# Layer 1's attention: first query inside the last expert step, activation tables asked for earlier, PSUM banks reordered and released singly

## The chip, the cores and the metric

The kernel runs on one core of a Trainium2 chip. The metric is the device time of one execution in microseconds; the time of a kernel is the median of several runs. A separate execution is recorded by the hardware profiler, and all profile lines come from that one. The core has five engines that work side by side, each in its own order: TensorE (PE, with its weight loads as PEld), VectorE (DVE), ScalarE (ACT), GpSimd (POOL) and SyncE (SP), which here only starts transfers. They wait for each other on semaphores.

## The reference

The input x has 8 batches of 512 tokens with 512 features, in fp32. Two layers follow, each an attention and a feed-forward block; after every block the sum of block and input is normalised over the features:

```python
x = _layernorm(x + L0_attn(x))   # causal softmax attention, 16 heads of 32, biases
x = _layernorm(x + L0_ffn(x))    # 8 experts, top 2 of a softmax router, LoRA on all weights
x = _layernorm(x + L1_attn(x))   # no mask, 8 query heads of 64 in 2 groups of one key/value head; returns x + out @ Wo.T
x = _layernorm(x + L1_ffn(x))    # silu(x Wg) * (x Wu), then Wd; weights are integers (w - 128) * scale, 1408 hidden
```

In layer 1's attention the scores are `softmax(q k^T / sqrt(64))`. An expert computes `silu(gate) * up` on 256 hidden features and projects them down to 512.

## The kernel before, in words

**Layer 0's attention** (`attention0`) goes through the batches in turn, and in each through four groups of four heads. A group is three units of scores: the scores on TensorE, Exp on ScalarE (L1470), the causal mask as a select on GpSimd (L1480), the product with v on TensorE (`av`, L1497), and the running sum of p on VectorE (L1505). At a group's end TensorE sums over the keys (`rs`, L1512), ScalarE copies that to `r_inv` (L1074), VectorE takes the reciprocal (L1515) and multiplies (L1516), and GpSimd adds the inverses into a guard, `g_total` (L1077). Once a batch GpSimd also adds a bias row to x (L1589).

**The experts.** Tokens are gathered into tiles of 128 by expert. `Tiles.step` (L1012) is the pipeline: step i starts the gate and up matmuls of a later tile, transposes the hidden values of tile i (`turn_hidden`, L968: two transposes into `ps_hT`, a copy to `hT` on ScalarE), and multiplies them by the down weights (`down`, L978: four passes into `ps_y`, a copy to `y` on ScalarE or VectorE, and a DMA from SP to `results`). The loop in `usual_pass` calls `step` and then a piece of other work meant for that step (`beside`), among them the pieces of layer 1's attention for batch 0: its gathers, sums and norm, its key, its value and, as the last piece, its first query (`query`, L1717: eight passes into `ps_q`, a copy to `qT`, L1724). After the loop, `rare` (L1036) has each engine read a tile count, `t_n_free` (L1039), and branch (L1041): extra tiles are computed only in the unusual case, which doesn't occur in this run.

**Layer 1's attention** (`Attention1.run`, `batches`) starts behind that branch. SP loads the rows of batches 2 to 7 (`load_rows`, L1954, two DMAs of 512 KB a batch); GpSimd gathers the expert results of the next batch (`yr`, L722), and VectorE adds them to x with their weights (L729). The attention itself is a stream of units: scores (two heads at a time, in banks of the pool `p_sc`), Exp to `p` on ScalarE (L1818), sums over the key tiles on VectorE (`total`, L1826), the product with v (`av`, L1837), and at a group's end `rs` (L1845, in a bank of the pool `p_mm`), the copy `r_inv` (L1074), reciprocal (L1848) and `aoT` (L1855). The projection with Wo (`ps_o`) is followed by the residual on VectorE (L1790), the statistics (L1798, L1799), `rstd` on GpSimd (L1802, L1803) and the norm (L1809).

For the last batch there is no next one beside which the projection could stand. Its four token tiles get four banks; each is first projected over three of the four groups, then over the last group, with residuals and then statistics behind (L1919 to L1934). The first two banks come from `p_mm`, the other two from `p_sc`.

**Layer 1's feed-forward** (`IntegerFfn.run`, L1191) opens its PSUM pools `d_gu` and `d_o` on the banks that the attention has given back, and computes for every chunk of 128 hidden features `ps_g` and `ps_u` (L1222), `sg` by Silu on ScalarE (L1225), `hT` on VectorE (L1227), its high and low halves (cast on ScalarE L1232, difference on VectorE L1233) and the down matmuls `ps_f` (L1238). The integer weights are converted on VectorE a slice at a time (L1137).

**What sets the order.** Inside `in_order(...)` blocks the named engines execute in the order in which the program issues their work: VectorE, ScalarE, GpSimd and SP in the loop over the expert steps, VectorE, ScalarE and GpSimd in layer 1's attention. Elsewhere a scheduler orders the instructions by their dependences. A tile pool with `reuse_waits="tile"` makes the first user of a place wait for the users of just that place; without it, for the last user of all the places that the pool takes over.

Of the kernel before, what the change touches and what calls it, by code (L numbers as in the profile page):

```python
# [9 lines left out]
F32 = mybir.dt.float32  # L10
# [3 lines left out]
AF = mybir.ActivationFunctionType  # L14
ALU = mybir.AluOpType
AX = mybir.AxisListType
PSUM = bass.MemoryType.PSUM

P = 128
NB = 8  # L20
S = 512
# [46 lines left out]
def in_order(tc, *engines):  # L68


    return tc.manual_schedule(engines={mybir.EngineType.PE, *engines})
# [43 lines left out]
class Env:  # L115
# [19 lines left out]
    def open_stream(self, ctx, batches, **kw):  # L135

        resident = ctx.enter_context(self.tc.tile_pool(name=f"resident{batches[0]}", bufs=1, **kw))
        for b in batches:
            self.xs[b] = resident.tile([P, NT, D], F32, tag=f"x{b}", name=f"x_{b}")
# [687 lines left out]
class Tiles:  # L827
# [181 lines left out]
        for i in range(2, 4):  # L1009
            self.turn_rows(i, self.nc.scalar.copy)  # L1010

    def step(self):  # L1012
        i = self.next
        self.next += 1
        if i == 0:
            self.down(i)
        if i + 2 < N_FIXED:
            self.half(i + 2)
        elif N_FIXED <= i + 1 < self.n:
            self.gate_up(i + 1, lambda: self.turn_hidden(i))  # L1020
        elif i + 1 == self.n:
            self.turn_hidden(i)
        if i + 8 < self.BY_BLOCKS:
            self.fetch(i + 8)
        if i + 10 >= self.BY_BLOCKS:
            self.fetch(i + 10)
        if i:
            self.down(i)
        for n in (4, 5) if i == 0 else (5,):
            if i + n < self.BY_BLOCKS:  # L1030
                self.turn_rows(i + n)
        if i + 6 >= self.BY_BLOCKS:
            self.pair_back(i + 6)
        if i + 7 >= self.BY_BLOCKS:
            self.blocks(i + 7)
# [109 lines left out]
class IntegerFfn:  # L1145
# [45 lines left out]
    def run(self, held_out, last_norm):  # L1191
        tc, nc, weights = self.env.tc, self.nc, self.weights
        with ExitStack() as phase:
            self.work = phase.enter_context(tc.tile_pool(name="d_work", bufs=1))
            self.p_gu = phase.enter_context(tc.tile_pool(name="d_gu", bufs=2, space=PSUM))
            self.p_o = phase.enter_context(tc.tile_pool(name="d_o", bufs=1, space=PSUM))
            weights.open(phase.enter_context(tc.tile_pool(name="d_weights", bufs=1)), 3 * NHID - weights.at)
            self.sd = self.work.tile([P, D], F32, name="sd")
            with tc.tile_pool(name="d_slots", bufs=1) as slots:
                while weights.at < 3 * NHID:  # L1200
                    weights.load(slots, 4, 3 * NHID)
                    weights.convert()
                nc.sync.dma_start(out=self.sd, in_=self.env.ins.s_down.partition_broadcast(P))
            with tc.tile_pool(name="d_raw", bufs=1) as self.raw:
                for b in range(NB - 1):
                    self.batch(b)
                    if b == 0:
                        last_norm()
                        ps = self.p_gu.tile([1, 1], F32, tag="g", name="ps_held")
                        nc.scalar.dma_start(out=held_out, in_=self.guard.partitions_held(self.env.const, ps))  # L1210
            self.late = phase.enter_context(tc.tile_pool(name="d_late", bufs=self.HELD))
            self.batch(NB - 1)
# [437 lines left out]
class Attention1:  # L1650
# [78 lines left out]
    def first_pieces(self):  # L1729

        do = self.first = self.prepare(0)

        def fetch(t):
            do["fetch"](t)
            self.scale(t)

        def blocks(tiles):
            for t in tiles:
                do["blocks"](t)

        return ([lambda t=t: fetch(t) for t in range(NT)] + [lambda t=t: do["add"](t) for t in range(NT)]
                + [do["deviations"], do["norm"], lambda: blocks((0, 1)), lambda: blocks((2, 3)), lambda: None, lambda: None]
                + [do["key"], do["value"], lambda: do["query"](0)])

    def scale(self, c):

# [12 lines left out]
    def batches(self, work, p_sc, p_av, weights, split):  # L1759
        env, nc, guard, state, HD = self.env, self.nc, self.guard, self.state, self.HD  # L1760
# [2 lines left out]

        state[0]["aoT"] = work.tile([P, ND, S], F32, tag="aoT", name="aoT1", bufs=2)
        weights.load(work, 2, weights.FIRST)

        w_out = work.tile([P, ND, 512], F32, name="attn1_out")
        for j in range(2):
# [6 lines left out]
        pieces = {0: self.first}  # L1775
# [7 lines left out]
        def project_groups(b, t, ps, groups):  # L1783
            for c in groups:
                self.multiply(1, ps, state[b]["aoT"][:, c, ts(t, P)], w_out[:, c, :], c)
# [136 lines left out]
        banks = [self.mm([P, D], "ps_o1")]  # L1922
        project_groups(b, 0, banks[0], range(ND - 1))
        sums[-1]()
        banks.append(self.mm([P, D], "ps_o1"))
        banks += [p_sc.tile([P, 2, S], F32, tag="sc", name="ps_o1")[:, 0, :] for _ in range(2)]
        for t in range(1, NT):
            project_groups(b, t, banks[t], range(ND - 1))
        norm(b - 1)
# [8 lines left out]
def usual_pass(tc, ins, held_out):  # L1938
    nc = tc.nc
    with ExitStack() as ctx:  # L1940
        env = Env(ctx, tc, ins)
        guard = Guard(env)
        keep = ctx.enter_context(tc.tile_pool(name="routed", bufs=1, side="right"))
        dram = ctx.enter_context(tc.tile_pool(name="routed_rows", bufs=1, space=bass.MemoryType.DRAM))
        with tc.tile_pool(name="a_mm", bufs=2, space=PSUM) as p_mm, ExitStack() as attn1_ctx:
            with tc.tile_pool(name="routes", bufs=1, side="right") as routes, \
                    tc.tile_pool(name="experts", bufs=1, side="right") as pool, ExitStack() as tiles_ctx:
                experts = Experts(env, pool, dram)
                router, tiles, tables = attention0(env, guard, keep, routes, experts, dram, p_mm, tiles_ctx)

                def load_rows(b):
                    for t in range(0, NT, GAP // P):
                        rows = router.rows[router.row_at(b, t) :][:GAP]
                        nc.sync.dma_start(out=env.xs[b][:, t : t + GAP // P, :], in_=rows.rearrange("(t p) d -> p t d", p=P))  # L1954

                env.open_stream(ctx, range(2))
                rows = ctx.enter_context(tc.tile_pool(name="c_rows", bufs=1))
                own = attn1_ctx.enter_context(tc.tile_pool(name="c_own", bufs=1))
                attention = Attention1(env, guard, router, rows, own, p_mm, dram)
                beside = {tiles.next + 6 * (b + 1): lambda b=b: load_rows(b) for b in range(2)}  # L1960

                for i, piece in enumerate(attention.first_pieces()):
                    beside[E * NT + 4 + 2 * i] = piece
                with in_order(tc, mybir.EngineType.DVE, mybir.EngineType.Activation, mybir.EngineType.Pool,
                              mybir.EngineType.SP):
                    while tiles.next < tiles.n:
                        tiles.step()
                        next(tables, None)
                        beside.pop(tiles.next, lambda: None)()
                assert not beside and next(tables, None) is None  # L1970
                tiles.rare()
            env.open_stream(ctx, range(2, NB), side="right")
            for b in range(2, NB):
                load_rows(b)
            weights = IntegerWeights(env, guard)
            pool = ctx.enter_context(tc.tile_pool(name="c_weights", bufs=1, side="right"))
            weights.open(pool, weights.FIRST)
            pool.tile([P, 56], F32, name="c_aligned")
            ffn = IntegerFfn(env, guard, weights, rows, dram)
            last_norm = attention.run(weights, ffn.split)  # L1980
        ffn.run(held_out, last_norm)
# [223 lines left out]
def post_ln_two_layers(tc, *aps):  # L2205

    nc = tc.nc  # L2210
    ins = Inputs(*aps)
    with tc.tile_pool(name="flag", bufs=1, space=bass.MemoryType.DRAM) as dram:
        held = dram.tile([1, 1], I32, name="held_out")
        usual_pass(tc, ins, held)
        count = nc.values_load(held[0:1, 0:1], min_val=0, max_val=P, skip_runtime_bounds_check_because="a count of partitions")
        with tc.If(count < P):
            general_pass(tc, ins)
# [70 lines left out]
```

## Time and profile before

| | us |
|---|---|
| median of 3 runs (2122.55 to 2125.76) | 2122.95 |
| the profiled execution | 2119.8 |
| its span, first to last instruction | 2118.1 |
| TensorE busy | 2080.9 |
| VectorE busy | 1269.7 |
| ScalarE busy | 606.6 |
| GpSimd busy | 498.2 |

The granted TensorE clock is 0.997 of full speed. Three places of the span matter for what follows: about 50 to 62 us (batch 0 of layer 0's attention), about 1071 to 1094 us (the last expert tile and the start of layer 1's attention), and about 1603 to 1630 us (the end of that attention and the start of the feed-forward block).

A line of a timeline has the start and the length in us, the engine, the source line and operation, what is written and read, and the number of instructions put together; in brackets stands how long the engine was idle before it and what it then waited for. A line of the waits has the engine and what waited, then what for, the us in total, the number of times and the longest. A line about DMA has the number of transfers, the size of each and the median time from issue to landing.

### The profile page before, as it was taken

What the parts mean: (1) busy time and instruction counts of PE and PEld (TensorE: products, weight loads), DVE (VectorE), ACT (ScalarE), POOL (GpSimd) and SP (SyncE); (2) the same over time, 40 slices, a digit from 0 to 9 for tenths busy, and PEclk for the clock granted to TensorE, in tenths of its full rate; (3) what the DMA queues carried; (4) which work ended last, traced back from release to release, by engine and by line L of the source; (5) the groups of instructions that cost most, each with busy time, mean ns of one, the idle gap of its engine ahead of it and who ended that gap; (6) DMA issues with size and microseconds to landing.
All of it is one profiled execution on the core that took longest, in us unless ns stands there. A gap on an engine that the chain in (4) does not pass through costs nothing. (4 is left out here: it accounts for less than half of the span.)

```text
span 2118.1 us, 35841 instructions
## 1 busy us (share of the span) xinstructions
PE 2080.9 (98%) x15114; PEld 1051.5 (50%) x15114; DVE 1269.7 (60%) x1963; ACT 606.6 (29%) x838; POOL 498.2 (24%) x489
## 2 busy tenths in 40 slices
PE   9999999999999999999999999999999999999997
PEld 2333333333334677774433333333334888888886
DVE  3667676776767633224247898887867644555443
ACT  2333323323323111111133333333332322222222
POOL 2343534434333211232042222223101000000000
PEclk9999999999999999999999999999999999999999
DMA  9020303414222447777561322132102311111000
GB/s 323 22 73 29 101 19 108 144 47 155 82 100 101 134 140 225 231 237 210 155 208 50 100 71 80 50 100 80 41 1 70 100 40 60 60 60 60 21 20 22
DMA packets 170588, 208.16 MB, mean 98 GB/s; under 512 B 61851, under 2 KB 115099, under 8 KB 167347
## 3 DMA queue, kind: packets, MB, share of 16 engines
q1 hardware_dynamic: 159136, 170.10, 25.6%
q0 software_dynamic: 10560, 34.61, 5.5%
q8 instruction: 122, 2.00, 0.4%
q10 hardware_dynamic: 722, 1.07, 0.1%
q14 instruction: 48, 0.39, 0.1%
HBM read 129.96 MB, written 75.78 MB: 97 GB/s over the span
## 5 line engine op out<-in xcount | busy, mean ns | idle before, releaser
L1077 POOL TENSOR_TENSOR g_total<-g_total,r_inv 128x512 f32<-128x512 f32 x64 | 90.1, 1408 | 487.3 <-DVE r_inv L1848 269.9
L1470 ACT ACTIVATE p<-sc 128x2048 f32<-128x2048 f32 (+1 forms) x96 | 153.0, 1593 | 178.9 <-PE sc L65 155.3
L1505 DVE TENSOR_TENSOR p<-p 128x1536 f32<-128x1536 f32 (+2 forms) x96 | 149.9, 1562 | 80.3 <-POOL p L1480 70.2
L1227 DVE SCALAR_TENSOR_TENSOR hT<-ps_u,vec,sg 128x512 f32<-128x512 f32 x88 | 65.6, 746 | 188.9 <-PE ps_u L1222 188.9
L1238 PE MATMUL ps_f<-ffn_w,h_half 128*128 128x512 f32 x672 | 169.8, 393 | 2.6 <-DVE h_half L1233 2.0
L957 PE MATMUL ps_gu<-xrT,experts 128*128 128x256 f32 x736 | 166.7, 380 | 0.0
L957 PEld LDWEIGHTS ps_gu<-xrT,experts 128*128 128x128 f32 x736 | 139.2, 191 | 31.9 <-issue 15.6
L1818 ACT ACTIVATE p<-sc 128x1024 f32<-128x1024 f32 x128 | 124.2, 1022 | 99.3 <-PE sc L65 99.3
L1848 DVE RECIPROCAL r_inv<-r_inv 128x512 f32<-128x512 f32 x32 | 107.1, 3346 | 67.6 <-ACT r_inv L1074 67.6
L1238 PEld LDWEIGHTS ps_f<-ffn_w,h_half 128*128 128x128 f32 x672 | 124.5, 188 | 34.6 <-DVE h_half L1233 7.6
L1222 PE MATMUL ps_g<-x_high,ffn_w 128*128 128x512 f32 x352 | 137.3, 390 | 0.8 <-DVE x L1790 0.8
L1222 PE MATMUL ps_g<-x_low,ffn_w 128*128 128x512 f32 x352 | 137.2, 390 | 0.0
L1222 PE MATMUL ps_u<-x_low,ffn_w 128*128 128x512 f32 x352 | 137.2, 390 | 0.0
L1222 PE MATMUL ps_u<-x_high,ffn_w 128*128 128x512 f32 x352 | 137.1, 389 | 0.0
L65 PE MATMUL sc<-qT,kT 64*64 64x512 f32 x1024 | 124.7, 602 | 1.1 <-ACT qT L1724 0.7
L65 PE MATMUL ps_q<-experts 128*32 128x512 f32 x1024 | 120.8, 601 | 4.8 <-DMA experts<-in_xT 4.4
L1480 POOL TENSOR_SCALAR_AFFINE_SELECT p<-p 128x512 f32<-128x512 f32 x128 | 82.7, 658 | 165.1 <-ACT p L1470 155.5
L65 PE MATMUL ps_v<-experts 128*32 128x512 f32 x1024 | 120.9, 595 | 0.0
L1837 PE MATMUL av<-p,v 128*64 128x512 f32 x512 | 120.9, 594 | 0.0
L65 PE MATMUL ps_o<-attn_out,aoT 128*64 128x512 f32 x512 | 116.4, 598 | 0.8 <-ACT r_inv L1074 0.8
L65 PE MATMUL ps_k<-experts 128*32 128x512 f32 x1024 | 116.3, 595 | 0.0
L65 PE MATMUL ps_q<-hT,attn_qkv 128*64 128x512 f32 (+1 forms) x504 | 116.2, 596 | 0.0
(277 smaller groups left out, 3198.0 us busy)
## 6 DMA issues: line engine op xcount, KB each, us to landing
results<-y SPq DMA_DIRECT2D x68, 256.0 KB, 2.7
turned<-turned SPq DMA_DIRECT2D x56, 256.0 KB, 4.1
pair<-xrT SPq DMA_DIRECT2D x25, 512.0 KB, 2.9
xrT<-pair SPq DMA_DIRECT2D x100, 128.0 KB, 3.8
x<-in_x SPq DMA_DIRECT2D x8, 1024.0 KB, 8.3
rows<-x SPq DMA_DIRECT2D x32, 256.0 KB, 2.4
x<-rows SPq DMA_DIRECT2D x16, 512.0 KB, 11.0
experts<-in_xT SPq DMA_DIRECT2D x7, 1024.0 KB, 8.7
```

Of the source, the lines that this page charges most:

```text
L65: nc.tensor.matmul(out[m], lhsT=lhsT[:, m], rhs=rhs, start=start, stop=stop)
L957: nc.tensor.matmul(ps[:, j, :], lhsT=w, rhs=xT[:, c, :], start=c == 0, stop=c == ND - 1)
L1077: self.nc.gpsimd.tensor_tensor(self.total, self.total, r_inv, ALU.add)
L1222: nc.tensor.matmul(ps, lhsT=w[:, ts(dc, P)], rhs=x[:, dc, :], start=(dc, i) == (0, 0), stop=(dc, i) == (ND - 1, 1))
L1227: nc.vector.scalar_tensor_tensor(hT, u, vec[:, V_SU + c : V_SU + c + 1], sg, ALU.mult, ALU.mult)
L1238: self.nc.tensor.matmul(os[t], lhsT=h[:, ts(t, P)], rhs=self.weights(2 * NHID + c), start=(c, i) == (0, 0), stop=(c, i) == (NHID - 1, 1))
L1470: nc.scalar.activation(p, sc[:, :, :width], AF.Exp, scale=scale)
L1480: nc.gpsimd.affine_select(out=first, in_=first, pattern=[[0, 4], [1, P]], compare_op=ALU.is_ge, fill=0.0, base=0, channel_multiplier=-1)
L1505: nc.vector.tensor_tensor(total[:, :, P * kt :], total[:, :, P * kt :], p[:, :, at : at + w], ALU.add)
L1818: nc.scalar.activation(p, sc, AF.Exp, scale=scale)
L1837: nc.tensor.matmul(st["av"][HD * j : HD * (j + 1), :], lhsT=st["v"][:, kt, HD * j : HD * (j + 1)], rhs=p[:, j, :], start=kt == 0, stop=kt ...
L1848: nc.vector.reciprocal(r_inv, r_inv)
```

## The change

The first query is no longer a piece beside the loop. `first_pieces` returns it apart, and `step` calls it as `amid`, in the last step only, between that tile's `turn_hidden` and its `down`. A one-column tile `spare` is added to the pool `small`; an Exp on it is issued at the start of `batches` and a Silu on it behind the last group's `sums[-1]()`. Of the last batch's four banks, the second `p_mm` bank moves from token tile 1 to token tile 3. The feed-forward block's two PSUM pools get `reuse_waits="tile"`.

```diff
-    def step(self):
+    def step(self, amid=lambda: None):
         i = self.next
...
         elif i + 1 == self.n:
             self.turn_hidden(i)
+            amid()
...
-            self.p_gu = phase.enter_context(tc.tile_pool(name="d_gu", bufs=2, space=PSUM))
-            self.p_o = phase.enter_context(tc.tile_pool(name="d_o", bufs=1, space=PSUM))
+            self.p_gu = phase.enter_context(tc.tile_pool(name="d_gu", bufs=2, space=PSUM, reuse_waits="tile"))
+            self.p_o = phase.enter_context(tc.tile_pool(name="d_o", bufs=1, space=PSUM, reuse_waits="tile"))
...
-                + [do["key"], do["value"], lambda: do["query"](0)])
+                + [do["key"], do["value"]]), lambda: do["query"](0)
...
         weights.load(work, 2, weights.FIRST)
+        spare = env.small.tile([P, 1], F32, name="spare")
+        nc.scalar.activation(spare, env.neg_half[:, :1], AF.Exp)
...
         sums[-1]()
+        nc.scalar.activation(spare, env.neg_half[:, :1], AF.Silu)
+        banks += [p_sc.tile([P, 2, S], F32, tag="sc", name="ps_o1")[:, 0, :] for _ in range(2)]
         banks.append(self.mm([P, D], "ps_o1"))
-        banks += [p_sc.tile([P, 2, S], F32, tag="sc", name="ps_o1")[:, 0, :] for _ in range(2)]
...
-                for i, piece in enumerate(attention.first_pieces()):
+                pieces, query = attention.first_pieces()
+                for i, piece in enumerate(pieces):
                     beside[E * NT + 4 + 2 * i] = piece
...
-                        tiles.step()
+                        tiles.step(query)
```

In the instruction orders as built, these are the differences. TensorE: the eight query passes stand ahead of the last `down`. ScalarE: the `qT` copy stands ahead of the last `y` copy and of the branch; the spare Exp stands at the start of the kernel, behind the first table load, and the table load ahead of layer 1's first `p` stays where it was; the Silu table load stands behind the last `r_inv` copy. GpSimd: the first `g_total` of batch 0 in layer 0 stands ahead of that batch's second addition of the bias row (to batch 1's x) instead of behind it. VectorE and SP keep their order. The buffers on the left side of SBUF that come behind the pool `small` start 64 bytes later.

## The prediction

> **What bounds the kernel.** I read the busy shares first, then TensorE's waits, then the timeline around each place that the change touches. TensorE is the bound:
>
> ```profile
> PE 2080.9 (98%) x15114; PEld 1051.5 (50%) x15114; DVE 1269.7 (60%) x1963; ACT 606.6 (29%) x838; POOL 498.2 (24%) x489
> ```
>
> It is idle for 2118.1 - 2080.9 = 37.2 us in all, and works in order, so a wait of its own that goes or comes moves the end by its length unless a later wait takes it up. The change adds no matmul. Its waits, in total us, times, longest:
>
> ```profile
> PE ps_g L1222 <- DVE x L1790: 0.8, 1, 0.8
> PE ps_o L65 <- ACT r_inv L1074: 0.8, 1, 0.8
> ...
> PE sc L65 <- ACT qT L1724: 0.7, 1, 0.7
> PE ps_f L1238 <- issue: 0.6, 1, 0.6
> PE ps_y L982 <- ACT hT L976: 0.5, 1, 0.5
> ```
>
> All five lie at two places, the start of layer 1's attention (place A) and its end (C): 3.4 us, or 0.16% of the span. That is the most that the change can be aimed at. A measurement of this kernel tells about 0.2% (4.2 us) from no change.
>
> **Place A: the query goes ahead of the last tile's down projection.**
>
> ```profile
> 1072.37 1.99 PE L982 MATMUL ps_y<-experts,hT 128*128 x4 [0.52 <-ACT hT L976]
> 1074.19 3.60 PE L65 MATMUL ps_q<-hT,attn_qkv 128*128 128x512 f32 x8
> ...
> 1078.93 0.95 POOL L722 DMA_INDIRECT yr<-results,r_results_i  x1 [0.83 <-issue]
> ...
> 1087.93 0.75 DVE L729 SCALAR_TENSOR_TENSOR x<-yr,r_weights,x 128x512 f32<-128x512 f32 x1 [0.34 <-DMA yr<-results,r_results_i]
> ...
> 1092.21 1.08 PE L1845 MATMUL rs<-total,ones 128*64 128x512 f32 x4 [0.37 <-DVE total L1826]
> ```
>
> After the change the eight query matmuls fill the 0.52 that `down` waited for hT; `down` then ends near 1077.0. The qT copy (0.58) runs during `down`, from about 1075.3, so the first scores wait only for the branch of the rare tiles. The row of before has them at 1078.46; now they start at about 1077.9, some 0.5 to 0.8 earlier.
>
> But everything behind `down` comes later. ScalarE's last y copy starts at 1074.43 in the trace; now it starts when `down` is done, at about 1077.1: +2.65. Queued behind it on ScalarE are the load of t_n_free and the branch (0.5 more), no hardship, since the first Exp wasn't due before. Queued behind it on SP are that tile's y DMA (issued 1075.04, landed 1077.04), SP's own load and branch (0.6 and more) and the twelve x<-rows loads of 512 KB. The y DMA moves to 1077.7 and lands near 1079.7. SP's first load of rows started at 1078.22 because SP waited for TensorE's branch; now, with the 0.97 that lay between that y's issue and SP's branch and some 0.9 of semaphores behind it, SP gets there about 1079.6, 1.3 later. GpSimd's gathers of yr wait for that y to land: the semaphores cleared at 1078.2 and the first gather's record stands 0.7 behind; now 1079.8 + 0.7 = 1080.5, +1.6.
>
> Who waits for the gathers? VectorE's order is written out: x<-yr (1086.84 and 1087.93), statistics, then the two totals (1089.55, 2.52), and the first `rs` waits for the totals. So TensorE has its 0.5 us early and then stands at `rs`, which moves with the second yr. If the gathers land 1.6 to 1.8 later, `rs` does too: **+1.7**. Lower bound -0.4: the landing doesn't move because the loads ahead of it are what holds it, and TensorE keeps what it gained less what `rs` waits for. Upper bound +4.1: the gather now stands 0.25 us later relative to the loads, and one more 512 KB load gets ahead of it. The loads landed at 1081.89, 1084.63, 1086.37, 1089.60 and 1093.08, about 2.8 us each. I take +1.7, the nearest to the issue times.
>
> The Exp table load of place A (1.28 us, at 1078.43) is not taken away. In the built order the spare Exp activation has been hoisted to the very start of the kernel, behind the first table load there, where ScalarE has nothing to do before 13.04; the load in front of layer 1's first p stays behind the branch. Cost and gain 0.
>
> **Place B, a side effect in layer 0.** With the spare in the program, the scheduler puts batch 0's first g_total ahead of x += row on GpSimd. Before:
>
> ```profile
> 51.49 4.56 POOL L1589 TENSOR_TENSOR x<-x,row 128x2048 f32<-128x2048 f32 x1
> 56.01 1.73 POOL L1077 TENSOR_TENSOR g_total<-g_total,r_inv 128x512 f32<-128x512 f32 x1
> 57.70 1.62 POOL L1480 TENSOR_SCALAR_AFFINE_SELECT p<-p 128x512 f32<-128x512 f32 x1
> ```
>
> ```profile
> 53.29 3.32 DVE L1505 TENSOR_TENSOR p<-p 128x512 f32<-128x512 f32 x1
> ```
>
> g_total needs the reciprocal, which ends at 53.37, so GpSimd now idles from 51.5 to 53.4, does g_total, then the 4.56 of x += row, then the select (0.63 alone) for which TensorE's av waits; av stood at 60.20. How these overlap with VectorE decides it. The Trainium skill (SBUF — State Buffer, "SBUF: two separate sides") says that a VectorE operation with two inputs in SBUF and a GpSimd operation exclude each other for the whole instruction. The rows: the VectorE add above takes 0.63 at 67.14 with GpSimd idle and 3.32 here, ending 0.6 after GpSimd's x += row. That is the rule, to the tenth. Without a lock: g_total 53.4 to 54.7, x to 59.2, select to 59.9, no stall. With it: VectorE's short add first (to 53.9), g_total to 55.2, then VectorE's add of 128x1024 (1.1) that has been waiting, to 56.3, then x to 60.7 and the select to 61.3, so av starts 1.1 late: **+1.1**. Bounds 0 (x takes its turn ahead of VectorE's add) and +1.5. Nothing later absorbs it: TensorE's next waits here are on the same chain.
>
> **Place C: attention's end.**
>
> ```profile
> 1607.32 11.38 PE L65 MATMUL ps_o<-attn_out,aoT 128*64 128x512 f32 x52 [0.84 <-ACT r_inv L1074]
> ...
> 1627.71 1.16 PE L1238 MATMUL ps_f<-ffn_w,h_half 128*128 128x512 f32 x4 [0.57 <-issue]
> ```
>
> The bank that waits for ScalarE's r_inv copy (done 1607.2) is now the last of four. Token tiles 1 and 2 start at once, so the projections start 1.0 earlier, at 1606.3. The FFN's first ps_g now waits for the first residual instead of all four and loses its 0.85 as well: about 1617.5 instead of 1619.54. But what is late next? The first ps_f (1627.71) hangs on VectorE: fourth residual, four statistics, GpSimd's rstd, norm (1624.16), a weight conversion (1.22), hT (1626.22), then ScalarE's cast (to 1627.61). VectorE's residuals follow the projections, and so that chain moves by 1.0 and no more; TensorE waits about 1.8 there. The Silu table load (1.28 at 1621.83) is moved ahead; it delayed the first sg to 1623.12, but hT at 1626.22 did not wait for it. Value **-1.0**, bounds -0.9 and -2.05 (both waits gone, if the chain is less tight than that).
>
> **The 64 bytes.** The spare tile moves every left-side buffer behind it by 64 bytes, among them yr and x of batches 0 and 1, which started at multiples of 256. The Trainium skill (DMA: Bandwidth & Descriptors, "How a descriptor splits into AXI transactions") says that a piece not starting at 256 bytes costs beats for the bytes in front: 2 beats in 66 for a 2 KB row, 3%, or 0.1 us on each of some forty transfers, none of them waited for except at A. The rows:
>
> ```profile
> rows<-x SPq DMA_DIRECT2D x32, 256.0 KB, 2.4
> ...
> out<-x SPq DMA_DIRECT2D x28, 256.0 KB, 2.3
> ```
>
> The first reads buffers at 160 beyond a multiple of 256, the second ones of several offsets, 8 of 28 at none; they take the same. By the rule up to +0.1 at A, by the rows 0. I take 0.
>
> **Sum and the rivals.** 1.7 + 1.1 - 1.0 = +1.8 us. The profiled execution took 2119.8 (span 2118.1), so it becomes 2121.6; the median of the runs is 2122.95, 3.15 above the profiled one, and becomes 2124.75, say **2124.7**.
> - *Likeliest, 0.81:* within 0.2%, the three parts nearly cancelling. Its own range is 2120.5 (A -0.4, B 0, C -2.05: -2.45) to 2127.1.
> - *Faster by over 0.2%, 0.05:* it would have to gain more than the 3.4 us at which it is aimed, at 2118.7 or less. Nothing in the waits speaks for it; only a wait that the trace does not show could.
> - *Slower by over 0.2%, 0.14:* yr falls behind more x<-rows loads. With one more, A is +4.1 or so and the sum about +4.2; with two, A is +6.9 and the sum +7.0: 2130. It decides from A = +4.15, that is when x<-yr starts later than 1092.1. For it: gathers and loads already share the DMA engines, the loads taking 3.7 to 13 us. Against it: both queues move by nearly the same, 1.3 and 1.6.
> - *It doesn't do what it says:* true of the Exp preload, at no cost. If A and C both come to nothing, only B is left, 2124.
>
> Range 2120.5 to 2128.0: the lower end from all lower bounds, the upper from A and B at their upper bounds (4.1 + 1.5 - 0.9 = 4.7).
>
> **What would show it.** In the changed profile: the waits ps_y<-hT, sc<-qT and ps_o<-r_inv gone; the first yr gather at 1080 or later; `rs` waiting 2 us for the totals; av in batch 0 waiting about 1 us for the select; ps_g starting 2 us earlier than before against the start of the projections' rs, and the first ps_f waiting near 1.8. It would be wrong if yr lands no later than before, or if TensorE loses over 3 us at a place named nowhere above.

## The result, and the profile after

The changed kernel takes 2127.66 us in the median of 22 runs (2122.57 to 2133.05); the kernel before, run beside it, 2122.98 (22 runs). The ratio is 1.0018, with a 95% interval of 1.0012 to 1.0024: some 3.8 us slower (2.5 to 5.1; the two medians alone lie 4.7 apart), about the 0.2% that can be told from no change. The time lies inside the predicted range, 0.3 us below its upper end; the cost is twice the +1.8 us of the sum or a little more.

The profiled execution took 2128.3 us (span 2126.6), 8.5 more than the profiled one of before, which lay 3 us under its own median. So the two profiles are compared place by place: how far does the same matmul, counted from the start, lie behind its counterpart of before? That distance is called the lag here.

| place (time before, us) | lag of after at its end | added there |
|---|---|---|
| first loads of weights (to 12) | 1.12 | 1.1 |
| place B (to 66) | 1.31 | 0.2 |
| layer 0 and the experts (to 1059) | 3.52 | 2.2 |
| place A to the first `rs` (1092) | 5.47 | 1.95 |
| just behind it (to 1100) | 7.11 | 1.6 |
| rest of the attention (to 1600) | 6.82 | -0.3 |
| place C (to 1640) | 5.89 | -0.9 |
| feed-forward (1640 to 2090) | 8.71 | 2.8 |

The first row comes and goes from profile to profile (0.07 to 1.5), and the third lies between -0.8 and 2.5 in the profiles below, most of them of kernels that leave those stages alone; a wait of 1.4 us for an expert's xrT is part of it, and is in only two of those. So these 3.3 us are not put down to the change. The rest is. TensorE is busy longer than before, which no step of the prediction foresaw:

```profile
PE 2087.2 (98%) x15114; PEld 1050.9 (49%) x15114; DVE 1266.5 (60%) x1963; ACT 607.4 (29%) x840; POOL 498.6 (23%) x489
```

The number of matmuls is the same and their busy time is 6.3 us longer, so some matmuls have become slower. Among TensorE's waits, those for hT, qT and r_inv at places A and C and that of ps_g for the residual are gone. Two have grown, from 0.4 and 0.6, two more stand at layer 1's first scores (one for the branch, one for p, which was 0.4), and one has shrunk:

```profile
PE rs L1848 <- DVE total L1829: 2.3, 1, 2.3
PE ps_f L1239 <- issue: 1.5, 1, 1.5
...
PE sc L65 <- ACT p L1821: 0.9, 1, 0.9
PE sc L65 <- ACTq L1042: 0.9, 1, 0.9
...
PE ps_f L1239 <- DVE h_half L1234: 0.3, 1, 0.3
```

The last of these in the kernel before:

```profile
PE ps_f L1238 <- DVE h_half L1233: 2.0, 7, 0.5
```

Place A, in the timeline:

```profile
1075.21 3.60 PE L65 MATMUL ps_q<-hT,attn_qkv 128*128 128x512 f32 x8
...
1078.65 1.88 PE L982 MATMUL ps_y<-experts,hT 128*128 x4
...
1084.21 0.95 POOL L722 DMA_INDIRECT yr<-results,r_results_i  x1 [3.38 <-DMA results<-y]
...
1093.40 0.75 DVE L729 SCALAR_TENSOR_TENSOR x<-yr,r_weights,x 128x512 f32<-128x512 f32 x1 [1.61 <-DMA yr<-results,r_results_i]
...
1097.68 1.49 PE L1848 MATMUL rs<-total,ones 128*64 128x512 f32 x4 [2.35 <-DVE total L1829]
...
1099.10 3.18 PE L65 MATMUL sc<-qT,kT 64*64 64x512 f32 x16
```

GpSimd's bracket names the link: the first gather waits for the last y to reach memory. Less the 3.52 that TensorE lay behind anyway, the gather starts 1.8 later (5.28 - 3.52), the second x<-yr 1.95 later, and `rs` as well. Ahead of `rs` nothing was won: the first scores start 0.6 early, and the wait for p takes that back (lag 3.49 at 1092 us, 3.52 ahead of place A). The last two rows show something else: `rs` takes 1.49 instead of 1.08 and the sixteen scores 3.18 instead of 1.95. The granted clock explains it (from:to, length, busy us and instructions, clock, DMA share, GB/s):

```profile
1096.00:1098.00 2.00, 0.32 (x2) 1.00 1.05 393
1098.00:1100.00 2.00, 2.00 (x8) 0.56 1.03 379
1100.00:1102.00 2.00, 2.00 (x16) 0.59 1.05 388
1102.00:1104.00 2.00, 2.00 (x14) 1.00 1.05 384
```

The clock falls to half behind the 2.35 us in which TensorE stood still, and is back 3.4 us later; that is the 1.6 us of the fifth row of the table. The Trainium skill (TensorE: Matmul & The Clock Gate, "What's actually happening") has the halving after at least one idle window of about 3.4 us, of a window that runs on its own. The 3.4 us agree; but this wait is shorter than a window, so the window need not be idle throughout. What decides stands with e12 below.

Place B, with GpSimd's and TensorE's lines:

```profile
54.58 1.59 POOL L1078 TENSOR_TENSOR g_total<-g_total,r_inv 128x512 f32<-128x512 f32 x1 [1.92 <-DVE r_inv L1516]
...
56.13 5.54 POOL L1590 TENSOR_TENSOR x<-x,row 128x2048 f32<-128x2048 f32 x1
...
61.62 1.81 POOL L1481 TENSOR_SCALAR_AFFINE_SELECT p<-p 128x512 f32<-128x512 f32 x3
...
62.31 1.06 PE L1498 MATMUL av<-p,v 128*32 128x512 f32 x8
```

This is the sequence of the prediction, 1.1 later throughout because of the first loads: g_total, then VectorE's long addition ahead of x += row (so the 5.54 instead of 4.56), then the select. av starts at 62.31, where 60.20 + 1.12 = 61.32 would have been no delay: 1.0 late. But the next scores are not. Before:

```profile
60.20 0.59 PE L1497 MATMUL av<-p,v 128*32 128x512 f32 x1
...
62.86 0.69 PE L65 MATMUL sc<-q,k 32*64 32x256 f32 x16
```

After:

```profile
64.17 0.69 PE L65 MATMUL sc<-q,k 32*64 32x256 f32 x16
```

That is 1.31 later, 0.2 beyond the 1.12.

### The profile page after: what moved, and what is told of

Its sections match the earlier page's. It is cut to its first block, busy times and chain, and to the rows that moved or that the text cites. A ratio compares the mean times of both kernels' runs of the same rounds, so it can differ in the third digit from the quotient of the medians.

```text
span 2126.6 us, 35844 instructions
## 1 busy us (share of the span) xinstructions
PE 2087.2 (98%) x15114; PEld 1050.9 (49%) x15114; DVE 1266.5 (60%) x1963; ACT 607.4 (29%) x840; POOL 498.6 (23%) x489
## 5 line engine op out<-in xcount | busy, mean ns | idle before, releaser
L1226 ACT ACTIVATE sg<-ps_g,vec 128x512 f32<-128x512 f32 x88 | 60.6, 689 | 204.7 <-PE ps_g L1223 204.6
```

## The experiments

All ratios are against the kernel before on the same chip, with 95% intervals.

| run | ratio | interval |
|---|---|---|
| e1, 64 bytes alone | 1.0014 | 1.0007 to 1.0020 |
| e2, after, realigned | 1.0007 | 0.9999 to 1.0015 |
| e3, query alone | 1.0014 | 1.0007 to 1.0021 |
| e4, banks and pools alone | 0.9993 | 0.9985 to 1.0002 |
| e5, weights shifted | 1.0040 | 1.0027 to 1.0054 |
| e6, x and h shifted | 1.0045 | 1.0029 to 1.0060 |
| e7, query, later yr additions | 1.0011 | 1.0003 to 1.0020 |
| e8, the same with banks and pools | 1.0008 | 1.0000 to 1.0017 |
| e9, weights, x and h shifted | 1.0002 | 0.9993 to 1.0010 |
| e10, rows later | 1.0001 | 0.9995 to 1.0008 |
| e11, rows later, query, banks, pools | 1.0003 | 0.9997 to 1.0010 |

**Where does the feed-forward stage lose 2.8 us?** The theory after the result: the spare tile's 64 bytes. The rival: a phase of TensorE's queue, set by chance or by the other edits. e1 is the kernel before with one unused tile:

```diff
         self.small = ctx.enter_context(tc.tile_pool(name="small", bufs=2))
+        self.small.tile([P, 1], F32, name="pad")
```

> The kernel before with one unused tile in the pool `small`, so that the left-side buffers move by 64 bytes and nothing else changes. In the profile of the changed kernel the feed-forward matmuls follow each other at 229 ns instead of 226.7 and lose about 3 us over 480. Theory 1 (the addresses do it: TensorE reads x_high, x_low, h_half and ffn_w1 64 bytes past a multiple of 256): 229 ns here too, about +3 us, ratio 1.0014. Theory 2 (the spacing is a phase of TensorE's queue that the other edits or chance set): 226.7 ns, ratio 1.0000.

The stage loses 2.8 us here too (lag 1.57 at 1600, 4.36 at 2090). e2 is the changed kernel with a tile of 24 columns in the same place, which moves the buffers back to multiples of 256.

> The changed kernel with 192 bytes more in the pool `small`, so that the same buffers again start at multiples of 256. Theory 1: 226.7 ns between feed-forward matmuls, and the time falls by 3 us against the changed kernel, to a ratio of 1.0003 to 1.0008 against the kernel before. Theory 2: 229 ns stays or not whatever the addresses, ratio 1.0018.

The stage loses nothing (lag 5.13 at 1640, 5.14 at 2090). The mean time of a matmul in the groups of costliest instructions shows it: before, after, e1, e2.

```profile
L1222 PE MATMUL ps_u<-x_low,ffn_w 128*128 128x512 f32 x352 | 137.2, 390 | 0.0
```

```profile
L1223 PE MATMUL ps_u<-x_low,ffn_w 128*128 128x512 f32 x352 | 138.3, 393 | 0.0
```

```profile
L1223 PE MATMUL ps_u<-x_low,ffn_w 128*128 128x512 f32 x352 | 138.3, 393 | 0.0
```

```profile
L1224 PE MATMUL ps_u<-x_low,ffn_w 128*128 128x512 f32 x352 | 137.0, 389 | 0.0
```

The 393 ns overlap with their neighbours; from start to start of ps_g and ps_u it is 226.8 ns in the mean before and in e2, and 225 to 241, in the mean 229.6, after and in e1 (ps_f 227.8 before, 228.8 after). Over some 2100 matmuls that is about 4.5 us; the waits for h_half, which shrank from 2.0 to 0.3, give 1.7 of it back. The addresses do it, and nothing else of the change does.

**Which address?** The first weight tile lies on the right side of SBUF and did not move. e5 moves only the weights by 64 bytes, e6 only x_high, x_low and h_half, with counter-pads that leave the rest in place. The edit of e5:

```diff
-            weights.open(phase.enter_context(tc.tile_pool(name="d_weights", bufs=1)), 3 * NHID - weights.at)
+            wide = phase.enter_context(tc.tile_pool(name="d_weights", bufs=1))
+            wide.tile([P, 16], F32, name="pad0")
+            weights.open(wide, 3 * NHID - weights.at)
+            wide.tile([P, 48], F32, name="pad1")
...
-            pool.tile([P, 56], F32, name="c_aligned")
+            pool.tile([P, 40], F32, name="c_aligned")
```

The edit of e6:

```diff
+        self.small.tile([P, 1], F32, name="pad")
...
-            weights.open(phase.enter_context(tc.tile_pool(name="d_weights", bufs=1)), 3 * NHID - weights.at)
+            wide = phase.enter_context(tc.tile_pool(name="d_weights", bufs=1))
+            wide.tile([P, 48], F32, name="pad0")
+            weights.open(wide, 3 * NHID - weights.at)
```

> The kernel before with the feed-forward weights (both tiles) 64 bytes past a multiple of 256, and x_high, x_low and h_half where they were. In ps_g and ps_u the weights are the operand that TensorE loads and x the one that it streams; in ps_f h_half is loaded and the weights are streamed. If the streamed operand's address matters: ps_g and ps_u stay at 226.7 ns, ps_f goes to 229 or more, about +1 to +2 us (672 of 2100 matmuls). If the loaded operand's matters: ps_g and ps_u at 229 ns or more, about +3 us, ps_f unchanged.

> The counterpart: x_high, x_low and h_half 64 bytes past a multiple of 256, both weight tiles at multiples of 256. If the streamed operand's address matters: ps_g and ps_u at 229 ns, ps_f unchanged, about +3 us. If the loaded operand's matters: ps_f alone slower, about +1 us. If neither alone does it, both this and the counterpart stay at 226.7 ns.

Both expectations failed: each half costs far more than the two together. All three products slow down in both (ps_g to 233 ns in e5 and 232 in e6, ps_f to 232 and 233), and the stage loses 8.8 and 7.9 us. That suggests that it is not where one operand lies, but how the loaded and the streamed one lie to each other. e9 tests that by moving all of them, the first weight tile too: e1's pad, and 40 columns in `c_aligned`.

> The kernel before with all operands of the feed-forward matmuls, both weight tiles included, 64 bytes past a multiple of 256. The two runs with one side shifted were each slower than the run with (nearly) both. Theory (what counts is how loaded and streamed operand lie to each other, not where each lies): 226.7 ns as in the kernel before, ratio 1.0000. Rival (each operand should start at a multiple of 256): 232 ns or more, ratio 1.004 or more.

From 1640 to 2090 us the lag stays at 4.99, and ps_u is as in the kernel before:

```profile
L1223 PE MATMUL ps_u<-x_low,ffn_w 128*128 128x512 f32 x352 | 136.9, 389 | 0.0
```

The theory holds: 64 bytes in common cost nothing. In the changed kernel x and the second weight tile moved, the first weight tile didn't, and that mismatch is the 2.8 us. The same traces say so once more: the last chunk's gate and up weights lie in the second tile, which moved with x, and after and in e1 its ps_u starts every 226.7 ns, where most chunks ahead of it take 229.3. Not explained is the 1.0 ns of ps_f, whose operands both moved. Why e1's mismatch of x with the first weight tile costs 2.6 ns a matmul where the same one in e6 costs 4 to 5 isn't settled, and no other distance than 64 bytes was tried.

**Place A.** e3 has the query ahead of the last `down` (the change's lines for `amid`, `first_pieces` and `step`) and nothing else.

> The query ahead of the last tile's down, without the spare tile, the banks and the pools; addresses as before. The theory of the prediction, with the size that the changed kernel's profile shows: the first `rs` of layer 1 stands for the totals, place A costs +3.3 to +3.6 us (ratio 1.0016). Rival, place A as the prediction took it: +1.7 (1.0008). Rival, the delay of place A was the 64 bytes or chance: 0 or a gain of up to 0.4 (0.9998).

```profile
1096.27 1.08 PE L1846 MATMUL rs<-total,ones 128*64 128x512 f32 x4 [2.44 <-DVE total L1827]
1097.28 1.95 PE L65 MATMUL sc<-qT,kT 64*64 64x512 f32 x16
```

The lag goes from 2.29 ahead of place A to 4.04 behind it: +1.75, the prediction's figure; the scores keep their 1.95, since the clock didn't fall behind these 2.44 us. The measured +3.0 us (1.5 to 4.5) allows both that and the larger figure with a fallen clock. In the kernel before `rs` already waited 0.37 for the gathers' totals, so the waits of 0.5 and 0.7 that the change took away ahead of it were not on the path at all.

e7 tests that link. It is e3 with VectorE's first yr additions one step later, behind the totals.

```diff
-                for t, i in ((0, 1), (1, 2)) if first else ((0, 0), (1, 1), (2, 1), (3, 2)):
+                for t, i in ((0, 2), (1, 2)) if first else ((0, 0), (1, 1), (2, 1), (3, 2)):
```

> The query ahead of the last down, as before in the run with the query alone, and in layer 1's first batch the additions of yr for token tile 0 one step later, so that VectorE's totals no longer stand behind them. Theory (TensorE's wait at `rs` comes from the gathers, through VectorE's order): the wait of 2.4 us at the first `rs` goes, and place A turns from +1.75 to between -1.3 and -0.6 against the kernel before (0.9994 to 0.9997 in time). Rival (the scores, the Exp or the branch are what is late): the wait stays above 1 us and the ratio near 1.0014.

At the first `rs` it does what the theory says: the lag falls from 0.30 to -0.60, a gain of 0.9. The time does not follow (expected 0.9994 to 0.9997): the lag is 2.60 soon after 1118 us, since the same y is waited for further on:

```profile
PE ps_hT L1689 <- DVE xn L763: 1.3, 1, 1.3
...
PE rs L1846 <- DVE total L1827: 0.6, 1, 0.6
```

The transposes of batch 1's norm, which waited 0.2 in the kernel before, now wait 1.3; with the 0.6 at the next `rs` that makes most of the +2.3. Some 0.7 is again the clock, which is 0.50 from 1116.75 to 1120.16 us. So the path is the gathers', not VectorE's order alone. The rival (scores or branch) falls too: the first `rs` wait did go. e8 adds the banks and pools.

> The same with the banks in the new order and the feed-forward pools released tile by tile, all addresses as before, no spare tile. Theory: place A -0.6 to -1.3 and place C -1.0, together about -2 us, ratio 0.9990, faster than both the kernel before and the changed one. Rival: the later yr additions bring a new wait at the norm or the turn of batch 1, and the sum is near -1.0 (0.9995).

Place A +2.6 (0.9 of it at half clock, from 1119.52 us), place C -1.0: the rival's reading, and worse than its sum.

**Place C.** e4 has the banks and the pools alone.

> The last batch's banks in the new order and the feed-forward pools released tile by tile, without the query and the spare tile. Theory: -1.0 us, ratio 0.9995, with the first ps_f waiting for the chain through VectorE. Rival (both waits gone for good): -2.05, ratio 0.9990.

The lag goes from 1.63 to 0.57: -1.05. The end of the chain is as predicted, and its wait of 0.57 has become 1.53:

```profile
1628.29 1.16 PE L1238 MATMUL ps_f<-ffn_w,h_half 128*128 128x512 f32 x4 [1.53 <-issue]
```

This is the fastest version tried; whether it beats the kernel before is not clear of noise.

**Could the gathers be faster?** e10 and e11 move the loads of rows into the first batch's later steps, with SP's order written out; e11 adds the query, banks and pools.

```diff
-            with in_order(self.env.tc, mybir.EngineType.DVE, mybir.EngineType.Activation, mybir.EngineType.Pool):
+            with in_order(self.env.tc, mybir.EngineType.DVE, mybir.EngineType.Activation, mybir.EngineType.Pool,
+                          mybir.EngineType.SP):
...
+                if first:
+                    for k in range(2, NB):
+                        todo[3 + (k - 2) // 2].append(lambda k=k: load_rows(k))
...
-            for b in range(2, NB):
-                load_rows(b)
```

> The kernel before with the loads of rows for batches 2 to 7 issued three steps later in layer 1's first batch, behind the gathers of yr instead of ahead of them. Theory (the gathers land 8 us after they start because they share the DMA engines with twelve loads of 512 KB): the first yr lands within 4 to 5 us, the first `rs` no longer waits for the totals, and the time falls by 0.4 to 0.6 us (0.9997). Rival (the gathers' own pace holds them): yr lands as late as before, ratio 1.0000.

> Later loads of rows together with the query ahead of the last down, the banks in the new order and the pools released tile by tile; addresses as before, no spare tile. Theory: with the gathers off the way place A gives what the change aimed at, -0.5 to -1.3, and place C -1.0: ratio 0.9990 to 0.9993. Rival (the y that comes later holds the gathers all the same): rs waits 1 us or more and the ratio is 0.9997 to 1.0003.

Neither shows a gain, and they don't tell whether the loads hold the gathers. SP has nothing to wait for, so in e10 it reached the loads at 1081.03, 0.8 us behind the first gather (1080.24) instead of 0.7 ahead, and yr landed as late as before. In e11 `rs` waited 3.4 us, place A cost 2.7 and C gave 1.05. That the loads hold the gathers is argued from their times; it is not shown.

**The changed kernel again.**

> The changed kernel once more, unaltered. In its first profile TensorE's granted clock fell to 0.56 for some 3.4 us behind the wait of 2.35 us at the first `rs`, in the run with the query alone it did not behind 2.44 us. If the fall is settled by the length of the wait, it is there again; if by where the wait falls, it may be missing, and place A is then +1.75 instead of +3.4. The feed-forward matmuls stand at 229 ns again.

It took 2126.46 us. `rs` waited 2.14, the clock fell to half, place A cost 3.1 (lag 1.82 to 4.92) and the feed-forward stage 2.8. The length of a wait doesn't settle whether the clock falls; where it lies does. In every profile that shows more than one fall, the falls lie whole multiples of 3.413 us apart (the changed kernel's, at 674.97 and 1098.22, 124.0 of them), and each lasts one such stretch or two, the last one at the program's end aside. Cut into these stretches, the profiles read:

| profile | TensorE's wait | busy in the stretch or stretches it lies in, of 3.41 us | clock in the next |
|---|---|---|---|
| after | 2.35 | 1.06 | 0.50 |
| e12 | 2.14 | 1.27 | 0.50 |
| e2 | 2.03 | 1.38 | 0.50 |
| e9, at the scores | 2.85 | 1.29, 2.68 | 0.50, 0.50 |
| e3 | 2.44 | 2.15, 2.22 | 1.00, 1.00 |
| e10, at the scores | 2.96 | 1.53, 2.33 | 1.00, 1.00 |
| e11 | 3.43 | 1.65, 1.74 | 1.00, 1.00 |

Where 2.0 us or more of the wait fall into one stretch the clock halves; where it is shared between two, 1.9 us or less in each, it doesn't, though it is longer in all. In all 14 profiles, from the first record of the full clock (by 10 us) on, every stretch at full clock with 1.4 us of matmuls or less was followed by the half clock; of 17 with 1.5 to 1.9 us three were (the falls of e7 and e8, beside transposes, are two of them), and of fuller ones none. Where between these the limit lies is open.

## Why the prediction was right, and where it was not

- **TensorE as the bound, and no gain:** right. It called for a time within 0.2%, slightly slower, and 1.0018 is that, near the edge. The median, 2127.66, lies above the 2127.1 that it gave this case.
- **A, +1.7:** right in mechanism and size. The first scores start 0.6 early (0.5 to 0.8 predicted), the gathers 1.8 later (1.6 predicted), and the first `rs` follows; e3 measures +1.75. Left out was what such a wait can bring with it: the halved clock, 1.6 more in both profiles of the changed kernel.
- **The Exp load stays behind the branch, Silu's is hidden:** right; the Exp load still stands between the first qT copy and the first p.
- **B, +1.1:** the term was mis-sized; it measured 0.2, in all three profiles that have the spare Exp (after, e2, e12), and nothing in the others. GpSimd and VectorE did just what the lock says, and av started 1.0 late. What failed is "Nothing later absorbs it": the sum took the start of av as the loss, and TensorE didn't stand there. In the kernel before those av passes had stretched among three query passes and the first of `rs`, from 60.20 on; in the changed one the query passes went ahead in one run and the eight av passes followed in 1.06 us. (The add of 0.63 at 67.14 that it compared with did not have GpSimd idle all through: a g_total starts at 67.37.)
- **C, -1.0:** right, -1.05 alone and -0.9 in the changed kernel. What is late next was named: the first ps_f, waiting 1.5 (1.8 predicted); the first ps_g starts 2.0 sooner behind `rs`, as predicted.
- **The 64 bytes, "By the rule up to +0.1 at A, by the rows 0. I take 0":** this step failed. Its estimates asked only what the shift does to transfers. No row of the kernel before could show what it does to TensorE, since there all operands of the feed-forward matmuls lay alike; but 2100 matmuls read the shifted buffers, and a bound from their number was not made. The stage loses 2.8 in e1 and e12 as after, and nothing in e2 and e9. The prediction's own sign of being wrong, a loss of over 3 us at a place named nowhere, was missed by 0.2.

Summed: A 1.75 + B 0.2 - C 1.0 + 2.8 = 3.75 without a fallen clock and about 5.4 with it; measured 3.8 (2.5 to 5.1). The clock fell in all three profiles that have the whole change (e2 among them); that it doesn't in every execution would fit the measured time, but isn't shown. That the range held is luck. The cost that the prediction missed and the one that it overrated lie on opposite sides, place A's upper bound was wide for another reason, and its upper terms sum to 4.7 us, that is 2127.65, which it rounded up to 2128.0; the median is 2127.66.

## What to carry to other kernels

Before removing a wait, follow the next one to its source: here TensorE's early start ended at a sum that waited for a gather, and the same edit had pushed that gather 1.8 us back. And a new tile in a shared pool moves every buffer behind it: look at what reads those buffers, and where matmuls follow each other as closely as here, try the loaded and the streamed operand at the same offset from a multiple of 256 bytes.

## What the runs showed of the hardware that was not expected

- The feed-forward matmuls, with weights and data in rounded fp32, start every 226.7 ns when both operands lie alike (both at a multiple of 256 bytes or both 64 behind), and every 229 to 233 ns in the mean where they differ by 64 bytes. Layer 1's attention, on slower fp32 passes, read shifted buffers too and lost nothing (lag 1.59 to 1.57 from 1097 to 1600 us in e1).
- The clock fell by half behind waits of 2.03 to 2.85 us of which 2.03 us or more lay in one stretch of 3.41 us, and not behind 2.44 to 3.43 us that were shared between two such stretches, 1.9 us or less in each.
- In e9 and e10 ScalarE stood still, some 6 us after the branch, for 6.1 and 4.7 us, in a stretch with the DMA engines fully busy, and the profile names no releaser that lies in the program. In e9:

```profile
1089.91 0.59 ACT L1725 COPY qT<-ps_q 128x512 f32<-128x512 f32 x1 [6.10 <-remote]
1090.55 3.69 PE L65 MATMUL sc<-qT,kT 64*64 64x512 f32 x16 [2.85 <-ACT qT L1725]
```

That execution of e9 lost 5.3 us there, in part because the clock was at half for 6.83 us behind it (the sixteen scores took 3.69 us instead of 1.95). The ratio of e9, 1.0002, speaks against most executions losing as much. The cause wasn't found.
